# Turning 19 of 41 row tiles on VectorE instead of TensorE

## The chip, the core and the metric

The kernel runs on one core of a Trainium2 chip. TensorE (PE in the profile) multiplies matrices, VectorE (DVE), ScalarE (ACT) and GpSimd (POOL) work on tiles in SBUF, and transfers are issued from the queues of SP, ACT and POOL. The metric is the time of one execution on the device in microseconds (us), smaller being better.

## The reference

The input x has 2708 rows of 1024 numbers in fp32, and adj is a 2708 x 2708 matrix of zeros and ones in which a row has about four ones. What is computed:

```python
h = maximum(layernorm(x), 0)
q, k, v = h @ W_q.T + b_q, h @ W_k.T + b_k, h @ W_v.T + b_v
z = (q @ k.T) / sqrt(1024) * adj
z = where(z == 0, -10000, z)
out = x + relu(softmax(z, axis=1) @ v)
```

Only the scores at edges count, except in rows without edges, so the kernel does not form q @ k.T as a whole. It forms M = W_q.T W_k, multiplies the rows of h by M, takes for each row the dot products with the rows of h at its edges, sums those rows with the softmax weights into u, and multiplies u by W_v.

## The kernel before, in words

Rows are worked on in tiles of 128, 22 in all, the last with 20 rows. There are four stretches of work, which overlap on different engines.

*The weights.* W_q and W_k are loaded in eight tiles of 128 rows each. TensorE forms M by a scheme of Strassen's kind with seven products of half blocks (`term`, L460, line L463; banks `ps_x`, `ps_y`, `ps_z`), ScalarE evicts it (`evicted`, L476), VectorE adds parts to it (`joined`, L479) and forms differences of its blocks, called T, in `wlow` (`ts_of_m`, L425, L431). The host gives each weight row in an order that is not that of the columns: column c * 128 + p stands at place 8p + c. Block c of M's rows is therefore the columns c * 128 to c * 128 + 127, read with a step of eight elements (`a_tile`, L451), and evictions put M's columns back in order (`place`, `taken`, L467 to L474).

*The search.* Tiles of adj are loaded, VectorE looks for the ones with `max_index` (`found`, L376), lists them (`listed`, L389 to L395), counts them (`counts`, L645 to L653), and sorts the rows by their number of edges (`sort`, L666 to L673, ending with `pos_i`). POOL writes each row's list of edges to its sorted place in DRAM (`put`, L613) and the table is read back (`reload`, L625). This is done twice: for tiles 8 to 21, and then for tiles 0 to 7. Meanwhile h is normalised tile by tile and stored in `h_dram` (L270).

*Units.* A loop runs over 20 units, each a pair of row tiles: units 0 to 9 multiply rows of h by M and give q, units 10 to 19 multiply rows of u by W_v and give the output; one row tile, number 8, is left alone at the end. A unit is again seven products of half blocks (`multiply`, L982, line L948), and it needs its rows turned, with the columns in the partitions. For this TensorE multiplies 128 x 128 blocks with an identity (`half_turned`, L397, L402, bank `pt`), ScalarE copies them out (`held`, L682, L684), and VectorE and POOL form four sums and differences, s1 to s4 (`put`, L686, L688). `blocks` gives two steps, `upper` and `lower`, which are called in the unit before at given steps i of `after(i)` (L1172). The tiles of units 0 to 3 are those of h as they lie in SBUF (`kept`, `natural_rows`); units 4 to 9 gather their rows in sorted order from `h_dram` (`load_rows`, L1130, tiles `qr`); units 10 to 19 take u either from SBUF (`held`) or, when it was ready three units ahead or more, from `u_dram`, to which it was stored (`near`, L933). Ten tiles went through `u_dram`: 6, 5, 4, 3, 2, 0, 1, 20, 18 and 19.

*Attention.* For each sorted tile POOL gathers rows of h, one for each edge (L597), VectorE takes dot products with q (`scores`, L826), and sums the gathered rows with their weights into u (`sums`, L879), the first of them by ScalarE (`weights`, L871). It is a stream of steps (`attention`, L897) that is advanced between the steps of the units, by a fixed share for each step (`advance`). The order of the tiles is 6, 5, 4, 3, 2, 0, 1, 7, 13, 12, 11, 10, 14, 9, 15, 16, 20, 17, 18, 19, 8.

The order of VectorE's instructions is that of the program from beginning to end, and so is that of ScalarE's until unit 4 (`manual_schedule`, L413, L1164) and of POOL's in parts. An instruction that waits holds up all that follow on its engine. TensorE, SP and the rest are ordered by a planner when the kernel is built. The steps of the search stand in two tables, `steps_at` and `steps_ahead` (L735 to L740), with unit and step as keys. The kernel's helper `owe` (L278) adds rows into `hsum` on POOL at times when VectorE is not working on two operands.

After the last unit a flag tells whether any row had more edges than there is room for; only then does a slow general version of the whole follow, which does not run with this input.

## Time and profile before

| | |
|---|---|
| time, median of 3 runs | 647.9 us (647.47 to 648.41) |
| span of the profiled execution, first to last instruction | 641.9 us |
| time beyond the span (median less span) | 6.0 us |
| TensorE busy | 635.2 us, 1731 matmuls |
| VectorE busy | 521.9 us |
| POOL busy | 377.3 us |
| ScalarE busy | 279.6 us |
| moved by DMA | 189.02 MB, 294 GB/s in the mean |

The profiled execution's own time is not listed beside its span; the three timed runs stand within 0.15% of each other, and their median less the span is taken as what lies around it. In rows of groups the columns are line, engine, operation, output and inputs with shapes and count, then the busy time in us and the mean of one in ns, then the idle time before them and who ended it. In a timeline they are start, length, engine, line, operation, and in brackets the idle time before. In a table of stages they are the stage, its length, and the busy time of PE, PEld (TensorE's weight loads), DVE, ACT and POOL with the numbers of instructions, the granted clock of TensorE, the share of the DMA engines and GB/s. In rows of waits they are the total, how many times, and the longest.

### The profile page before, as it was taken

The page shows a single profiled execution, that of the slowest core. Times are in us where ns is not written, and L with a number is a line of the kernel's source. Part 1 is how long each engine was busy: PE and PEld are TensorE (multiplying, and loading weights), DVE is VectorE, ACT ScalarE, POOL GpSimd, SP SyncE. Part 2 cuts the span into 40 slices and gives each one's busy share as a digit, 9 for nine tenths or more (in the row PEclk, how much of TensorE's full clock was granted, in tenths as well). Part 3 has the DMA queues.
Part 4 walks back from the last instruction along what each step waited for, and adds up shares of the span by engine and source line. Part 5 has one row for each costly group of instructions (what it writes and reads, how often), then busy time and mean ns, then how long its engine had stood idle before and what let it go on. Part 6 is the DMA issues. An engine that isn't in the chain of part 4 may idle for free.

```text
span 641.9 us, 6381 instructions
## 1 busy us (share of the span) xinstructions
PE 635.2 (99%) x1731; PEld 326.2 (51%) x1731; DVE 521.9 (81%) x1014; ACT 279.6 (44%) x426; POOL 377.3 (59%) x400
## 2 busy tenths in 40 slices
PE   9999999999999999999999999999999999999996
PEld 5777766444544444444444454454454444444442
DVE  5999788997895755998888959997999989989121
ACT  3539974849775622423223132433342344333300
POOL 2649960875858457755735525665685856872431
PEclk9999999999999999999999999999999999999999
DMA  8999997598798969998977998988898989995542
GB/s 338 407 366 314 345 346 295 189 358 301 264 358 317 363 201 404 355 359 257 322 260 275 419 416 267 327 272 255 240 328 272 283 331 304 281 285 125 146 139 95
DMA packets 61986, 189.02 MB, mean 294 GB/s; under 512 B 10701, under 2 KB 11037, under 8 KB 61048
## 3 DMA queue, kind: packets, MB, share of 16 engines
q0 software_dynamic: 27888, 84.95, 41.6%
q1 hardware_dynamic: 29994, 89.36, 37.7%
q10 hardware_dynamic: 4062, 14.24, 5.9%
q8 instruction: 16, 0.26, 0.2%
q14 instruction: 26, 0.21, 0.1%
HBM read 159.81 MB, written 42.31 MB: 315 GB/s over the span
## 4 chain that ended last, share of the span: by engine, by line
PE 98%; DMA 1%; DVE 0%; POOL 0%; POOLq 0%; issue 0%
PE ps L948 45%; PE psy L948 32%; PE ps_y L463 6%; PE pt L402 6%; PE ps_x L463 4%; PE ps_z L463 4%; DMA wlow<-in_wq_dram 1%; PE ps_h L1153 0%; PE ps_v L581 0%; DVE y_alone L1297 0%; POOL out_dram L1281 0%; POOLq L1303 0%; PE ps_all L664 0%; PE ps_in L662 0%; PE ps_b L728 0%
## 5 line engine op out<-in xcount | busy, mean ns | idle before, releaser
L597 POOL DMA_INDIRECT g<-h_dram,tab x105 | 124.8, 1188 | 70.4 <-ACT u L871 19.1
L948 PE MATMUL ps<-M,a 128*128 128x512 f32 x320 | 144.0, 593 | 0.0
L948 PE MATMUL psy<-wlow,s 128*128 128x512 f32 x320 | 143.9, 592 | 0.0
L826 DVE SCALAR_TENSOR_TENSOR junk<-g,pq 128x1024 uint8<-128x1024 f32 x93 | 114.0, 1226 | 9.8 <-DMA g<-h_dram,tab 7.3
L879 DVE SCALAR_TENSOR_TENSOR u<-g,coef,u 128x1024 f32<-128x1024 f32 x79 | 101.4, 1283 | 5.6 <-ACT u L871 3.7
L948 PEld LDWEIGHTS ps<-M,a 128*128 128x128 f32 x320 | 59.3, 190 | 68.0 <-issue 67.4
L948 PEld LDWEIGHTS psy<-wlow,s 128*128 128x128 f32 x320 | 59.2, 190 | 66.8 <-issue 65.8
L376 DVE FIND_INDEX8 at<-ones,adj 128x8 uint32<-128x685 f32 (+1 forms) x88 | 74.5, 865 | 0.0
L948 PE MATMUL psy<-wlow,a 128*128 128x512 f32 x160 | 71.9, 592 | 0.0
L948 PE MATMUL ps<-M,s 128*128 128x512 f32 x160 | 71.9, 592 | 0.0
L948 PE MATMUL ps<-wlow,s 128*128 128x512 f32 x160 | 71.9, 592 | 0.0
L355 ACT ACTIVATE sized<-adj 128x2708 uint8<-128x2708 f32 (+1 forms) x22 | 54.3, 2468 | 7.7 <-DMA adj<-in_adj_dram 6.4
L285 POOL TENSOR_TENSOR hsum<-hsum,x 128x256 f32<-128x256 f32 (+1 forms) x56 | 38.6, 726 | 26.3 <-DVE wlow L431 22.3
L1047 POOL DMA_INDIRECT y<-in_x_dram,tab x19 | 33.5, 1763 | 30.8 <-ACT taken L1013 11.2
L948 PEld LDWEIGHTS psy<-wlow,a 128*128 128x128 f32 x160 | 30.4, 190 | 38.3 <-issue 37.8
L948 PEld LDWEIGHTS ps<-wlow,s 128*128 128x128 f32 x160 | 30.4, 190 | 38.3 <-issue 37.6
L948 PEld LDWEIGHTS ps<-M,s 128*128 128x128 f32 x160 | 30.3, 190 | 38.1 <-issue 37.4
L778 POOL DMA_INDIRECT out_dram<-y,tab x21 | 28.4, 1353 | 19.3 <-DMA y<-in_x_dram,tab 11.6
L684 ACT COPY a<-pt 128x512 f32<-128x512 f32 x60 | 33.4, 590 | 3.1 <-PE pt L402 3.1
L597 POOL DMA_INDIRECT M<-h_dram,tab x20 | 24.2, 1212 | 13.4 <-ACT u L871 4.7
L688 DVE TENSOR_TENSOR s<-a,pt 128x512 f32<-128x512 f32 x40 | 25.6, 681 | 7.8 <-ACT a L684 7.8
L871 ACT ACTIVATE u<-g,coef 128x1024 f32<-128x1024 f32 x16 | 18.4, 1149 | 27.1 <-DVE coef L870 26.3
(238 smaller groups left out, 847.9 us busy)
## 6 DMA issues: line engine op xcount, KB each, us to landing
adj<-in_adj_dram SPq DMA_DIRECT2D x21, 1354.0 KB, 12.0
x<-in_x_dram SPq DMA_DIRECT2D x21, 512.0 KB, 8.0
h_dram<-x ACTq DMA_DIRECT2D x21, 512.0 KB, 7.2
q_late<-q SPq DMA_DIRECT2D x12, 512.0 KB, 6.9
pq<-q_late SPq DMA_DIRECT2D x12, 512.0 KB, 4.8
u_dram<-u SPq DMA_DIRECT2D x10, 512.0 KB, 6.5
or<-u_dram SPq DMA_DIRECT2D x10, 512.0 KB, 8.2
g<-in_wv_dram SPq DMA_DIRECT2D x16, 256.0 KB, 8.3
```

The lines of the kernel that those rows point to most:

```text
L285: small.append(nc.gpsimd.tensor_add(hsum[:n, cols], hsum[:n, cols], xt[:n, cols]))
L355: nc.scalar.activation(sized[:n], a[:n, :, :PW], AF.Abs, accum_out=total[:n, t:t + 1])
L376: nc.vector.max_index(at[:n, k - first_k, g, :], ones[:n, 0:8], a[:n, g, :])
L402: nc.tensor.transpose(pt[:, c, :], xt[:, k * P:(k + 1) * P], ident)
L463: mm = nc.tensor.matmul(bank, a_tile(o + H * a[0], a[1], i), b(o), start=first and o == 0, stop=(o == H - 1), skip_group_check=True)
L597: return nc.gpsimd.indirect_dma_start(out=dst, out_offset=None, in_=src, in_offset=off, bounds_check=N - 1, oob_is_err=False)
L684: nc.scalar.copy(ops[name], bank)
L778: to = nc.gpsimd.indirect_dma_start(out=out, out_offset=bass.IndirectOffsetOnAxis(ap=ptab.bitcast(U32)[:n, t, SLOTS:SLOTS + 1], axis=0), i ...
L826: chained(lambda: nc.vector.scalar_tensor_tensor(junk, g_of[t][s], 1.0, tq[t], op0=ALU.mult, op1=ALU.mult, accum_out=zall[:, t, s:s + 1]))
L879: chained(lambda: nc.vector.scalar_tensor_tensor(u, g_of[t][s], coef[:, at[t][s]:at[t][s] + 1], u, op0=ALU.mult, op1=ALU.add))
L948: mm = nc.tensor.matmul(bank, a[:, c, :], b[:, c, :], start=False, stop=(c == 3), skip_group_check=True)
L1047: return nc.gpsimd.indirect_dma_start(out=y[:n], out_offset=None, in_=x, in_offset=off, compute_op=ALU.add)
```

## The change

Nineteen row tiles are no longer turned by TensorE. VectorE turns them in blocks of 32 x 32 with its own transpose (`faces`). Since such a block stays within 32 partitions, the rows come by four loads, one for each quarter of the partitions (`by_quarters`): quarter a gets columns 256a to 256a + 255 of all 128 rows, 32 rows side by side. The transpose reads every eighth column, so that partition p of block c holds column 8p + c. The weights are given plainly, and with the same step of eight as before their block c is now the columns 8p + c; M is evicted without being put in another order.

- Tiles 0 to 7 of h, in units 0 to 3, are loaded by quarters from `h_dram` (`quarter_rows`), not taken from SBUF. Both tiles of unit 0 are turned whole, ahead of part of `ts_of_m`; the others by halves.
- Tiles 6, 5, 4, 3, 2, 0, 1, 20, 18, 19 and 8 of u (`FACED`) are loaded by quarters from `u_dram`. Ten of them were stored and loaded before; tile 8 was not.
- The 12 tiles of units 4 to 9 come by gathers. ScalarE puts their columns in the order of the blocks (`combed`), and TensorE turns them as before. The other ten tiles of u are put in that order as they are summed (`combing`): u is written, and read back, at a step of 128 elements.
- s2 and s4 are formed by POOL for every pair with a tile that VectorE turned, in units 1 to 3 and in six of the later pairs; before, by POOL in units 1 and 2 alone. In unit 0 VectorE forms them, as before.
- `upper` and `lower` are called at other steps in units 0 to 2.
- `steps_at` is unchanged.

```diff
-P = 128
+P = 1024
+LANES = 128
+QUADS = 4
+FACED = (6, 5, 4, 3, 2, 0, 1, 20, 18, 19, 8)
+    def by_quarters(dst, rows):
+        faced.append(dst)
+        for a in range(QUADS):
+            cols = slice(a * D // QUADS, (a + 1) * D // QUADS)
+            nc.sync.dma_start(dst[a * QP:(a + 1) * QP, :].rearrange("r (g j) -> r g j", g=QUADS),
+                              rows[:, cols].rearrange("(g r) j -> r g j", r=QP))
+        return dst
+    def faces(dst, xt, lo, hi):
+        return nc.vector.transpose(dst.rearrange("p c (g r) -> p g c r", r=QP),
+                                   xt.rearrange("p (g r c) -> p g c r", g=QUADS, c=DC)[:, :, lo:hi])
+    def combed(xt, name):
+        c = row_tile(name)
+        nc.scalar.copy(c.rearrange("p (c q) -> p c q", c=DC), xt.rearrange("p (q c) -> p c q", c=DC))
+        return c
+    def combing(u, t):
+        return apart(u) if t in FACED else u.rearrange("p (c q) -> p q c", c=DC)
...
         def upper():
-            held("a11", half_turned(xa, 0))
-            held("a12", half_turned(xa, 1))
+            xa, xb = rows
+            if whole:
+                for xt, pair in ((xa, ("a11", "a12")), (xb, ("s3", "a22"))):
+                    wide = work.tile([P, D], FT, tag="q", name="turned", bufs=4).rearrange("p (c q) -> p c q", q=P)
+                    faces(wide, xt, 0, DC)
+                    ops[pair[0]], ops[pair[1]] = wide[:, :4], wide[:, 4:]
+                return
+            for s, name in enumerate(("a11", "a12")):
+                if is_faced(xa):
+                    faced_half(name, xa, s)
+                else:
+                    held(name, half_turned(xa, s))
...
-        ts_of_m(0, 0)
-        ts_of_m(1, 0, 1, 2, 3)
+        quarter_rows(0)
+        ts_of_m(0, 1)
         follow("i7.0-1")
+        ops_of[0] = blocks(rows_of.pop(0), whole=True)
+        ops_of[0][1]()
+        ts_of_m(2)
...
-ops_of[0][1]()
 ops_of[0][2]()
 banks_of = {0: banks_for(bp_sb)}
-    ts_of_m(0, 1, 3, 2)
+    ts_of_m(3)
...
             chained(lambda: nc.vector.scalar_tensor_tensor(
-                u, g_of[t][s], coef[:, at[t][s]:at[t][s] + 1], u, op0=ALU.mult, op1=ALU.add))
+                v, apart(g_of[t][s]), coef[:, at[t][s]:at[t][s] + 1], v, op0=ALU.mult, op1=ALU.add))
...
-                if i == (3 if n == 0 else 4 if turn else 0):
-                    ops_of[n + 1] = blocks(*rows_of[n + 1], nc.gpsimd if n + 1 < FIRST - 1 else None)
+                if i == {0: 3, 1: 3, 2: 2, FIRST - 1: 4}.get(n, 0):
+                    ops_of[n + 1] = blocks(rows_of[n + 1], nc.gpsimd if n + 1 < FIRST - 1 or any(
+                        is_faced(xt) for xt in rows_of[n + 1]) else None)
-                if i == (4 if n == 0 else 5 if turn else 2):
+                if i == {0: 4, 1: 4, 2: 3, FIRST - 1: 5}.get(n, 2):
                     ops_of[n + 1][2]()
...
+                if nxt[0] == "q" and n + 1 >= FIRST:
+                    if i == (3 if n + 1 == FIRST else 1):
+                        rows_of[n + 1][1] = combed(rows_of[n + 1][1], "cr")
+                    if n + 1 == FIRST and i == 2:
+                        rows_of[n + 1][0] = combed(rows_of[n + 1][0], "cr")
+                if i == 6 and n + 2 < len(units) and n + 2 > FIRST and units[n + 2][0] == "q":
+                    rows_of[n + 2][0] = combed(rows_of[n + 2][0], "cr")
```

176 lines of the change are left out of this document (91 added, 85 removed).

## The prediction

> **What bounds the kernel now.** I read the page's first parts for the bound, then the chain of waits in order of time, then each engine stage by stage for what comes just in time. Times are in us, from the start of the span.
>
> ```profile
> span 641.9 us, 6381 instructions
> PE 635.2 (99%) x1731; PEld 326.2 (51%) x1731; DVE 521.9 (81%) x1014; ACT 279.6 (44%) x426; POOL 377.3 (59%) x400
> ```
> ```profile
> 505.88 0.87 PE pt L402 x8
> ```
> ```profile
> 619.16 3.60 PE L948 MATMUL ps<-M,T_alone 128*128 128x512 f32 x8
> ```
>
> The first fence is the page, the second one row of the chain of waits, the third one of TensorE's timeline. TensorE is never without work, 99% of the span, and the turns of a row tile (pt, 8 of them, 0.87) lie in the chain. So an instruction taken from it is worth its full length, as long as everything else comes earlier by as much. The question is whether the others can. The runs had 647.47 to 648.41, median 647.9: 6.0 above the span. My sums are made on the span, and 6.0 is added.
>
> Two places have almost no slack. The first is the search for edges. Its table must be in DRAM before the rows of unit 4 can be gathered:
>
> ```profile
> 157.89 0.17 DVE L673 CAST pos_i<-deg 128x14 uint32<-128x14 f32 x1
> ...
> 192.70 1.07 POOL L599 DMA_INDIRECT qr<-h_dram,tab  x1 [2.38 <-DMA h_dram<-x]
> ```
> ```profile
> 200.43 1.05 PE L402 MATMUL pt<-ident,qr 128*128 128x128 f32 x8
> ...
> 205.63 1.88 PE L948 MATMUL ps<-M,a 128*128 128x512 f32 x4
> ```
> ```profile
> DMA to landing us min/median/max: 7.6/8.3/9.7
> ```
> ```profile
> 113.50:158.40 44.90, 44.90 (x126) 21.08 (x126) 40.36 (x110) 34.92 (x43) 34.34 (x59) 1.00 0.78 274
> 345.50:503.00 157.50, 157.50 (x446) 75.46 (x445) 140.83 (x213) 52.25 (x94) 93.27 (x71) 1.00 0.93 313
> ```
>
> The gather issued at 192.70 lands after 7.6 at the soonest, at 200.3, and TensorE turns its rows at 200.43: the slack is 0.1. Back from there it is one chain: table writes on POOL, the rows of the last tiles normalised and stored, all behind pos_i at 157.89. VectorE (third engine column of the stages) works 40.36 of 44.90 ahead of that, so pos_i comes when VectorE is through.
>
> The second place is the attention sums, 140.83 of 157.50 on VectorE. The last sum of tile 9 and of tile 8:
>
> ```profile
> 499.03 3.93 DVE L879 SCALAR_TENSOR_TENSOR u<-g,coef,u 128x1024 f32<-128x1024 f32 x3
> ...
> 590.13 1.28 DVE L879 SCALAR_TENSOR_TENSOR u<-g,coef,u 128x1024 f32<-128x1024 f32 x1
> ```
>
> Tile 9 is ready at 502.96 and turned at 505.88: slack 2.9. Tile 8 is ready at 591.4, its first block at 619.2.
>
> **The change, part by part.** *TensorE.* 19 tiles x 0.87 = 16.5 go: 8 in units 0 to 3, 7 (6.1) for the pairs of tiles 6,5 to 1,7, and 4 (20, 18, 19, 8; 3.5) at the end. If nothing waits: 631.4.
>
> *The price of a turn on VectorE.* No row shows one. It reads every eighth fp32 element, a stride of 32 bytes.
>
> ```profile
> L672 DVE TENSOR_REDUCE deg<-sort 128x14 f32<-128x252 f32 x1 | 0.6, 591 | 0.0
> L672 DVE TENSOR_REDUCE deg<-sort 128x8 f32<-128x144 f32 x1 | 0.4, 416 | 0.0
> L517 DVE TENSOR_SCALAR acc_b<-wlow,bq_sb 128x1024 f32<-128x1024 f32 x1 | 0.8, 753 | 0.0
> L688 DVE TENSOR_TENSOR s<-a,pt 128x512 f32<-128x512 f32 x40 | 25.6, 681 | 7.8 <-ACT a L684 7.8
> L431 DVE TENSOR_TENSOR wlow<-M,wlow 128x1024 f32<-128x1024 f32 x4 | 4.9, 1222 | 0.1
> ```
>
> L672 reads SBUF at strides of 56 and 32 bytes: (591 - 416) / (252 - 144) = 1.62 ns an element and 183 fixed, so a half tile of 512 takes 1.01 and a whole one 1.84. L517, one dense operand, is the cheap end: 0.75 a tile. I take L672, the row with the stride.
>
> *Search chain.* Unit 0 turns two whole tiles (3.7), units 1 and 2 four halves each (8.1): 11.8 ahead of pos_i. One L431 more comes ahead of the searches behind it (1.2). And VectorE waits, in order, for the first loads by quarters:
>
> ```profile
> 100.68 0.87 DVE L376 FIND_INDEX8 at<-ones,adj 128x8 uint32<-128x685 f32 x1
> ```
> ```profile
> 87.36 1.06 ACTq L270 DMA_DIRECT2D h_dram<-x  x2
> ```
> ```profile
> adj<-in_adj_dram SPq DMA_DIRECT2D x3, 1354.0 KB, 14.1
> h_dram<-x ACTq DMA_DIRECT2D x6, 512.0 KB, 3.6
> ```
> ```profile
> u_dram<-u SPq DMA_DIRECT2D x10, 512.0 KB, 6.5
> or<-u_dram SPq DMA_DIRECT2D x10, 512.0 KB, 8.2
> ```
>
> The stores of h end at 88.4 + 3.6 = 92.0. A load that takes 8.2 is there at 100.2, one that shares the queue with the adj loads (14.1) at 106.1; VectorE comes at 101.5. The wait is 0 to 4.6, and I take 2.5. Behind it on VectorE stand the searches, bp_sb and s1; behind the eight issues on SP the next adj loads, which VectorE does not need while it is itself late. Of the 4.5 idle before 158.4 I let 3.5 be used up. pos_i comes 2.5 + 11.8 + 1.2 - 3.5 = 12.0 later (2.2 with 0.75 a tile and no wait; 17.6 with the full wait and no idle used). Under this TensorE also loses its 7.0 of units 0 to 3: it gets to unit 4 early or on time, and waits.
>
> *Combing.* Rows from gathers are now first rearranged by ScalarE, 12 tiles. For unit 4 this stands in ScalarE's fixed order, so that behind the wait for the gather come the copies that free and fill the PSUM banks.
>
> ```profile
> 197.20 0.59 ACT L1026 COPY q<-ps 128x512 f32<-128x512 f32 x1 [2.85 <-PE ps L948]
> 197.68 1.11 ACT L713 COPY ps<-bp_sb 128x512 f32<-128x512 f32 x2
> 198.72 2.46 ACT L355 ACTIVATE sized<-adj 128x2708 uint8<-128x2708 f32 x1
> 201.09 0.19 ACT L355 ACTIVATION_READ_ACCUMULATOR sized<-adj 128x1 f32 x1
> 201.18 1.06 ACT L684 COPY a<-pt 128x512 f32<-128x512 f32 x2
> ```
> ```profile
> L871 ACT ACTIVATE u<-g,coef 128x1024 f32<-128x1024 f32 x16 | 18.4, 1149 | 27.1 <-DVE coef L870 26.3
> ```
>
> From the landing: comb 1.15, L1026 0.59, L713 1.11, comb 1.15, L355 2.65, first L684 0.53, together 7.2. Before it was 205.6 - 200.3 = 5.3. So unit 4 opens 12.0 + 1.9 = 13.9 late (4.1 to 19.5), and the attention stream with it: its own table is made from L688 of the same unit onward. The later combs are hidden by ScalarE's idle time (44% busy); without it each costs 1.15.
>
> *Attention stream.* From 345.5 to 503 VectorE gets 7 tiles x 2.02 = 14.1. The sums s2 and s4 of four pairs go to POOL: -8 x 0.69 = -5.5. But POOL's operations hold up VectorE's with two operands:
>
> ```profile
> 32.60 3.84 POOL L543 TENSOR_TENSOR wq<-wq,wlow 128x512 f32<-128x512 f32 x2 [3.45 <-DMA adj<-in_adj_dram]
> ```
> ```profile
> 33.02 5.83 DVE L519 SCALAR_TENSOR_TENSOR acc_b<-wk,bq_sb,acc_b 128x1024 f32<-128x1024 f32 x3
> ```
>
> Three operations of the kind that takes 1.28 alone (L879 above) took 5.83 beside two POOL operations: +1.0 for each, +8.0 for eight. POOL itself is 59% busy and hides the work; uncovered, each gather behind is 1.9 late (3.84 / 2). Of the waits in that stretch
>
> ```profile
> DVE junk L826 <- DMA g<-h_dram,tab: 7.3, 5, 2.1
> DVE s L688 <- ACT a L684: 3.4, 2, 2.2
> DVE u L1063 <- PE ps L948: 1.7, 1, 1.7
> ```
>
> a later VectorE meets none: -12.4. Net 4.2. The low end is 0 (an early VectorE still waits for its gathers). The sums of the ten tiles that TensorE still turns now read and write u at a stride of 512 bytes; I take 1.28 each, as now, and put the high end under the rivals.
>
> *Costed at nothing.* M is evicted straight, in as many instructions or fewer, in a stretch whose end TensorE sets. The weights' rows lie 32 KB apart instead of together, still 4 KB each: 0 to a few tenths at the start. The copies from PSUM that ScalarE no longer makes free an engine that is busy 44%. Loads by quarters have four issues and 1 KB runs; for tiles 6 to 1 and 20, 18, 19 they replace loads that are there (x10 above), well ahead of use.
>
> *Sum.* Tile 9 is ready 13.9 + 4.2 later, its slack of 2.9 is used, and the four last turns give 3.5 back: 13.9 + 4.2 - 2.9 - 3.5 = +11.7. The span is 653.6 and the time 659.6; I say 660. What is late next is the wait for u in the pair 14,9, while VectorE runs full.
>
> **The rivals.**
>
> *The turns hide, and it is faster.* With 0.75 a turn and no wait for the first loads unit 4 opens 4.1 late. The stream adds 0: 4.1 - 2.9 - 3.5 = -2.3, 645.6; if the sums too come in time, 4.1 - 9.6 = -5.5, 642.4. It decides in the search, ahead of pos_i: faster by over 0.2% needs delay and net stream work under 6.4 - 1.3 = 5.1 together. For it speak L517 and the 4.5 idle before 158.4; against it 40.36 of 44.90 and the slack of 0.1.
>
> *Strided sums.* At L672's rate a sum takes 1.84, not 1.28. Tiles 7, 13, 12, 11, 10, 14 and 9 have 2, 4, 4, 5, 5, 3 and 6 sums: 29 x 0.56 = 16.2 on a full engine. Then 659.6 + 16.2 = 675.8. The weight loads speak for it:
>
> ```profile
> L463 PEld LDWEIGHTS ps_y<-wlow 128*128 128x128 f32 x64 | 20.0, 313 | 7.4
> L948 PEld LDWEIGHTS ps<-M,a 128*128 128x128 f32 x320 | 59.3, 190 | 68.0 <-issue 67.4
> ```
>
> L463 takes its columns 32 bytes apart, L948 side by side: 313 against 190 ns. Against it: no row shows an operation with two operands at such a stride, and writes may not suffer. [...]
>
> *Tile 8 comes last.* It now goes through DRAM. VectorE ends it at 591.4 + 18.1 + some 5 (three more tiles turned) = 614.5; store 6.5, load 8.2, turn 1.84: 631.0. TensorE gets there at 619.2 + 15.2 - 2.6 = 631.8, just behind. With a load that takes 14.1 it waits 5.1 and the time is 664.7.
>
> **How the numbers follow.** About 0.2%, 1.3 us, is what a measurement of this kernel can tell from no change. Forecast (650 to 664) 0.43; tile 8 last 0.10; strided sums 0.25; faster 0.18; within 0.2% 0.04. So faster 0.18, same 0.04, slower 0.78. The range, 643 to 684, leaves out about 0.1 on each side; the forecast's own is 650 to 664.
>
> **What would show it.** Right: a gap on TensorE before its first turns of gathered rows, pos_i near 170, combs on ScalarE that wait for the gather, turns near 1.0 for 512, VectorE close to 100% from 350 to 500, TensorE waiting for u. Wrong: turns of 0.4, pos_i before 162, a chain that is still TensorE from end to end. L879 with a form at 1.8 would make it the second rival.

## The result, and the profile after

| kernel | median, us | lowest to highest | ratio to before, 95% interval |
|---|---|---|---|
| before | 648.15 | 647.47 to 649.79 | 1 |
| changed | 708.23 | 706.35 to 709.88 | 1.093 (1.0904 to 1.0956) |

The change is 9.3% slower, 60 us. The profiled execution of the changed kernel took 706.35 us with a span of 704.6, so 1.75 lies around the span and not 6.0: the profiled execution of before, with its span of 641.9, was some 4 us shorter than the timed ones.

The page after: its span, its busy times, and the granted clock in the 40 slices of the span:

```profile
span 704.6 us, 6216 instructions
PE 642.9 (91%) x1579; PEld 316.3 (45%) x1579; DVE 587.8 (83%) x1027; ACT 296.0 (42%) x408; POOL 417.9 (59%) x414
PEclk9999997999979999999999989999999899999999
```

The 152 blocks are gone from TensorE (1731 to 1579), and yet it is busy for longer: 642.9 after 635.2. Taken with the 16.5 us that were removed, the remaining work has become 24.2 slower. Idle it was for 641.9 - 635.2 = 6.7 and is now for 704.6 - 642.9 = 61.7. These two, 7.7 and 55.0, are the whole 62.7 by which the span grew. What TensorE waited for (us in total, times, longest):

```profile
PE ps L989 <- DVE s L470: 12.3, 3, 5.3
PE ps L989 <- DVE a L454: 9.7, 1, 9.7
PE psy L989 <- ACT taken L1054: 7.8, 6, 3.3
PE psy L989 <- DMA wlow<-tv_dram: 4.7, 1, 4.7
PE pt L406 <- DVE u L920: 4.7, 2, 4.4
...
PE pt L406 <- ACT cr L752: 3.7, 3, 2.3
```

TensorE's waits of this kind add up to 56.0 us. VectorE itself ended 36.2 of them, copies of ScalarE 13.9. How the lateness grew, read from the timelines of both kernels at the same places:

| place | before | after | later by |
|---|---|---|---|
| pos_i of tiles 8 to 21 | 157.89 | 173.12 | 15.2 |
| gather of unit 4's rows issued | 192.70 | 212.25 | 19.6 |
| first turn of unit 4 | 200.43 | 223.07 | 22.6 |
| first turn of unit 9 | 319.20 | 346.94 | 27.7 |
| first turn of the pair 13,12 | 449.84 | 485.52 | 35.7 |
| first turn of the pair 15,16 | 527.20 | 588.44 | 61.2 |
| end of the span | 641.9 | 704.6 | 62.7 |

So three stretches matter most: units 0 to 3 (22.6), the gathered rows (5.1), and the units of u, above all between the pairs 13,12 and 15,16 (25.5). TensorE's gaps in the first stretch, from its timeline (start, length, what, and in brackets the idle time before and who ended it):

```profile
108.47 5.37 PE L989 MATMUL ps<-M,turned 128*128 128x512 f32 x8 [3.92 <-DVE turned L454]
119.13 5.60 PE L989 MATMUL ps<-wlow,s 128*128 128x512 f32 x8 [5.30 <-DVE s L470]
...
162.28 0.27 PE L726 MATMUL ps_in<-sort,before 128*128 128x252 bf16 x1 [3.21 <-DVE sort L714]
...
199.87 6.19 PE L989 MATMUL ps<-M,a 128*128 128x512 f32 x8 [9.74 <-DVE a L454]
...
223.07 1.04 PE L406 MATMUL pt<-ident,cr 128*128 128x128 f32 x8
```

The gaps are 3.9, 5.3, 3.2 and 9.7, and each of the three long ones is followed by a block that takes 5.4 to 6.2 in place of 3.60. At unit 4 itself (the last row) TensorE does not wait at all. The costliest rows of VectorE and ScalarE that are new or have changed, from the groups:

```profile
L920 DVE SCALAR_TENSOR_TENSOR u<-g,coef,u 128x1024 f32<-128x1024 f32 x79 | 128.4, 1625 | 9.1 <-ACT u L911 7.2
L911 ACT ACTIVATE u<-g,coef 128x1024 f32<-128x1024 f32 x16 | 25.0, 1560 | 33.0 <-DVE coef L910 27.6 <-DVE m L909 5.2
L752 ACT COPY cr<-qr 128x1024 f32<-128x1024 f32 x12 | 24.8, 2067 | 27.6 <-DMA qr<-h_dram,tab 27.6
L920 DVE SCALAR_TENSOR_TENSOR u<-M,coef,u 128x1024 f32<-128x1024 f32 x13 | 21.0, 1614 | 2.4 <-ACT u L911 2.1
L454 DVE STREAM_TRANSPOSE a<-or 128x512 f32<-128x512 f32 x16 | 17.0, 1088 | 0.0
L454 DVE STREAM_TRANSPOSE turned<-hq 128x1024 f32<-128x1024 f32 x2 | 4.0, 2016 | 6.2 <-DMA hq<-h_dram 6.2
```

The means of L920 and L911 mix two kinds: sums of tiles in FACED take 1.28, those of the other ten tiles some 2.02, as this row of VectorE's timeline shows (six in a row, 12.13):

```profile
545.27 12.13 DVE L920 SCALAR_TENSOR_TENSOR u<-g,coef,u 128x1024 f32<-128x1024 f32 x6
```

### The profile page after: what moved, and what is told of

Read it like the earlier page. It is cut to its first block, busy times and chain, and to the rows that moved or that the text cites. A ratio compares the mean times of both kernels' runs of the same rounds, so it can differ in the third digit from the quotient of the medians.

```text
span 704.6 us, 6216 instructions
## 1 busy us (share of the span) xinstructions
PE 642.9 (91%) x1579; PEld 316.3 (45%) x1579; DVE 587.8 (83%) x1027; ACT 296.0 (42%) x408; POOL 417.9 (59%) x414
## 4 chain that ended last, share of the span: by engine, by line
DVE 36%; PE 22%; issue 16%; DMA 13%; ACT 5%; POOL 5%; SPq 1%; ACTq 0%; another core or an unknown queue 0%; POOLq 0%; DVEq 0%
DVE u L920 11%; DVE junk L858 8%; PE ps L989 7%; PE psy L989 5%; DVE at L380 4%; PE ps_x L540 4%; DMA adj<-in_adj_dram 3%; DMA g<-h_dram,tab 3%; DMA qr<-h_dram,tab 3%; DVE s L470 3%; DVE a L454 2%; PE ps_y L540 2%; PE ps_z L540 2%; POOL g L662 2%; DMA tv_dram<-g 2%
## 5 line engine op out<-in xcount | busy, mean ns | idle before, releaser
L662 POOL DMA_INDIRECT g<-h_dram,tab x105 | 136.1, 1296 | 72.6 <-ACT u L911 29.6
L989 PE MATMUL ps<-M,a 128*128 128x512 f32 x304 | 141.5, 609 | 9.7 <-DVE a L454 9.7
L920 DVE SCALAR_TENSOR_TENSOR u<-g,coef,u 128x1024 f32<-128x1024 f32 x79 | 128.4, 1625 | 9.1 <-ACT u L911 7.2
L858 DVE SCALAR_TENSOR_TENSOR junk<-g,pq 128x1024 uint8<-128x1024 f32 x93 | 116.7, 1255 | 4.0 <-DMA pq<-q_dram,tab 1.4
L989 PE MATMUL ps<-wlow,s 128*128 128x512 f32 x160 | 77.5, 630 | 12.3 <-DVE s L470 12.3
L1088 POOL DMA_INDIRECT y<-in_x_dram,tab x19 | 35.3, 1856 | 20.8 <-ACT y L1105 9.9
L911 ACT ACTIVATE u<-g,coef 128x1024 f32<-128x1024 f32 x16 | 25.0, 1560 | 33.0 <-DVE coef L910 27.6
L752 ACT COPY cr<-qr 128x1024 f32<-128x1024 f32 x12 | 24.8, 2067 | 27.6 <-DMA qr<-h_dram,tab 27.6
L662 POOL DMA_INDIRECT M<-h_dram,tab x20 | 26.1, 1306 | 13.7 <-ACT u L911 5.6
L746 ACT COPY ps<-bp_sb 128x512 f32<-128x512 f32 x42 | 24.6, 595 | 16.2 <-DVE bp_sb L652 7.9
```

The lines of the kernel that those rows point to most:

```text
L662: return nc.gpsimd.indirect_dma_start(out=dst, out_offset=None, in_=src, in_offset=off, bounds_check=N - 1, oob_is_err=False)
L752: nc.scalar.copy(c.rearrange("p (c q) -> p c q", c=DC), xt.rearrange("p (q c) -> p c q", c=DC))
L858: chained(lambda: nc.vector.scalar_tensor_tensor(junk, g_of[t][s], 1.0, tq[t], op0=ALU.mult, op1=ALU.mult, accum_out=zall[:, t, s:s + 1]))
L911: nc.scalar.activation(combing(u, t), apart(g_of[t][0]), AF.Copy, scale=coef[:, at[t][0]:at[t][0] + 1])
L920: chained(lambda: nc.vector.scalar_tensor_tensor(v, apart(g_of[t][s]), coef[:, at[t][s]:at[t][s] + 1], v, op0=ALU.mult, op1=ALU.add))
L989: mm = nc.tensor.matmul(bank, a[:, c, :], b[:, c, :], start=False, stop=(c == 3), skip_group_check=True)
```

## The experiments

All times are medians, and the ratio is to the kernel before on the same chip. What a part is worth is taken from the ratios, times 648.15, unless the text says that it goes by medians.

| run | what | us | ratio, 95% interval |
|---|---|---|---|
| e1_sums | changed, sums plain | 679.99 | 1.0464 (1.0442 to 1.0487) |
| e2_rows | changed, gathered rows not rearranged | 704.61 | 1.0845 (1.0821 to 1.0870) |
| e3_first | changed, units 0 to 3 turned by TensorE | 690.29 | 1.0622 (1.0583 to 1.0660) |
| e4_layout | plain weights alone | 649.82 | 1.0003 (0.9986 to 1.0020) |
| e5_u_faces | plain weights, 11 tiles of u turned by VectorE | 657.17 | 1.0129 (1.0101 to 1.0156) |
| e6_queue | changed, loads of h on ScalarE's queue | 722.51 | 1.1125 (1.1096 to 1.1153) |
| e7_order | changed, sums of unit 0 ahead of the search | 709.51 | 1.0938 (1.0914 to 1.0961) |
| e8_last_faces | plain weights, tiles 20, 18, 19 | 650.50 | 1.0028 (1.0008 to 1.0047) |
| e9_loads | plain weights and unused loads of h | 652.98 | 1.0063 (1.0041 to 1.0084) |
| e10_turns | plain weights and unused turns | 654.61 | 1.0087 (1.0061 to 1.0113) |
| e11_fewer | e5 without tiles 4 and 3 | 654.27 | 1.0096 (1.0067 to 1.0125) |
| e12_late | plain weights, tiles 18, 19, 8, turned late in order | 647.21 | 0.9983 (0.9973 to 0.9994) |
| e13_ahead | changed, turns of unit 3 ahead of the search | 707.46 | 1.0914 (1.0861 to 1.0967) |
| e14_vector | e5, s2 and s4 by VectorE | 654.60 | 1.0095 (1.0066 to 1.0123) |
| e15_prices | e4 and 21 single operations | 672.8, once | |
| e16_full | e12 and tile 20 | 655.76 | 1.0103 (1.0080 to 1.0127) |

### The parts taken back one at a time

Sums plain (`apart` leaves the order as it is). TensorE turns a tile by every eighth column, unless its columns were rearranged (`in_blocks`):

```diff
 def combing(u, t):
-    return apart(u) if t in FACED else u.rearrange("p (c q) -> p q c", c=DC)
+    return apart(u)
...
 def half_turned(xt, s):
...
-            nc.tensor.transpose(pt[:, c, :], xt[:, k * P:(k + 1) * P], ident)
+            block = xt[:, k * P:(k + 1) * P] if any(xt is y for y in in_blocks) else \
+                xt.rearrange("p (q c) -> p q c", c=DC)[:, :, k]
+            nc.tensor.transpose(pt[:, c, :], block, ident)
```

> The changed kernel, but u is summed plainly for all tiles (no step of 128 elements), and TensorE reads the ten tiles that it still turns by every eighth column. Theory A (the sums at a step of 512 bytes cost the most behind unit 12): every sum takes 1.28 again, VectorE loses 31 us of busy time, and most of the lateness that grew from 36 to 61 us between the pairs 13,12 and 15,16 goes: 708 becomes 676 to 690. Rival B (VectorE is full there by the turns and by POOL's s2 and s4, the sums only share the blame): no more than 10 us come back, 698 or more. If TensorE's turns suffer from the step of 32 bytes, up to 10 us are lost again and the rows of the turns show it.

It fell from 1.093 to 1.0464, by 4.7% or 30 us, inside Theory A's range. VectorE's rows of the sums in this run:

```profile
L923 DVE SCALAR_TENSOR_TENSOR u<-g,coef,u 128x1024 f32<-128x1024 f32 x79 | 106.2, 1344 | 8.9 <-ACT u L914 7.0
L923 DVE SCALAR_TENSOR_TENSOR u<-M,coef,u 128x1024 f32<-128x1024 f32 x13 | 16.7, 1283 | 1.5 <-ACT u L914 1.2
```

They take 122.9 where the changed kernel takes 149.4: 26.5 less VectorE, and about as much less time. In the changed kernel VectorE is busy 182.74 of the 190 us from 400 to 590, and TensorE, which was busy all the time before, 166.72:

```profile
400.00:590.00 190.00, 166.72 (x404) 74.78 (x403) 182.74 (x245) 60.95 (x96) 122.69 (x79) 0.93 0.83 256
```

The traced execution of this run is the slowest of its five (688.91); even there the pair 15,16 is 42.6 late and not 61.2.

Rows of units 4 to 9 straight from the gathers, turned by TensorE as above:

```diff
-                if nxt[0] == "q" and n + 1 >= FIRST:
-                    if i == (3 if n + 1 == FIRST else 1):
-                        rows_of[n + 1][1] = combed(rows_of[n + 1][1], "cr")
...
-                    rows_of[n + 2][0] = combed(rows_of[n + 2][0], "cr")
```

> The changed kernel without the rearranging of the gathered rows by ScalarE: TensorE turns the 12 tiles of units 4 to 9 by every eighth column. Theory A (lateness before unit 4 comes from units 0 to 3, the combs add only what the lateness grows from unit 4 to unit 9, 22.6 to 27.7): about 5 us come back, 700 to 706. Rival C (the chain gather, comb, turn is what opens unit 4 late, as the prediction had it): unit 4 opens 2 or more earlier and with it all behind, the gain is 2 to 4 at unit 4 and up to 12 x 2.07 = 25 in all.

1.0845, so 0.85% or 5.5 us come back (3.6 by the medians), on either side of the 5.1 in the table of lateness: Theory A. The much larger gain of Rival C is not there.

Units 0 to 3 from the rows in SBUF, as before the change:

```diff
-        quarter_rows(0)
         ts_of_m(0, 1)
         follow("i7.0-1")
-        ops_of[0] = blocks(rows_of.pop(0), whole=True)
-        ops_of[0][1]()
...
-                    quarter_rows(n + 2)
+                    natural_rows(n + 2)
```

> The changed kernel, but units 0 to 3 take the rows of h from SBUF again and TensorE turns them (every eighth column); no loads of h by quarters. Theory A (the gaps of 3.9, 5.3, 3.2 and 9.7 us in units 0 to 3 and the slower first blocks behind them make unit 4 22.6 late, and all of it is carried to the end): 708 becomes 682 to 689. Rival D (VectorE is the bound from 345 to 600 in any case and takes most of the gain back): 695 to 706.

1.0622: 3.1% or 20 us (17.9 by the medians). 690.29 lies between the two ranges, 1.3 above Theory A's and 4.7 below Rival D's: most of what units 0 to 3 lose, 22.6 by the table, is carried to the end.

All three, and nothing turned by VectorE:

```diff
-FACED = (6, 5, 4, 3, 2, 0, 1, 20, 18, 19, 8)
+FACED = ()
...
-                faces(uT, single["rows"], 0, DC)
+                for s in range(2):
+                    nc.scalar.copy(uT[:, 4 * s:4 * s + 4], half_turned(single["rows"], s))
```

> No tile is turned by VectorE, no row is rearranged, no sum is written apart: what is left of the change is the plain order of the weights, and TensorE turns all 41 tiles by every eighth column. Theory A (the three causes above are all there is): 646 to 652, like the kernel before. Rival E (the plain weights or the step of 32 bytes under TensorE's turns cost by themselves): 653 or more, and the rows of the weights' loads or of the turns are longer than before.

649.82, ratio 1.0003: the plain weights cost nothing that the interval of 0.2% to either side can show. TensorE's weight loads when it turns columns 32 bytes apart (first row, this run) and columns side by side (second row, the kernel before), and those of `term`, which read at a step of 32 bytes in both kernels (last row, this run):

```profile
L410 PEld LDWEIGHTS pt<-ident,qr 128*128 128x128 f32 x96 | 12.4, 191 | 7.2 <-issue 7.2
L402 PEld LDWEIGHTS pt<-ident,qr 128*128 128x128 f32 x96 | 11.1, 141 | 5.9 <-issue 5.9
L540 PEld LDWEIGHTS ps_y<-wlow 128*128 128x128 f32 x64 | 20.1, 313 | 7.4
```

With the step these loads take 191 and not 141. They run beside the matmuls, and a turn of eight blocks takes TensorE hardly longer, 1.04 to 1.06 and not 1.04. What makes the loads of `term` 313 stays open. Neither the rearranging by ScalarE nor the sums at a step were needed for TensorE's sake.

### The turns of u

What was left of the change beside those three parts, by itself (the diff is from e4):

```diff
-FACED = ()
+FACED = (6, 5, 4, 3, 2, 0, 1, 20, 18, 19, 8)
...
-                for s in range(2):
-                    nc.scalar.copy(uT[:, 4 * s:4 * s + 4], half_turned(single["rows"], s))
+                faces(uT, single["rows"], 0, DC)
```

> Only the eleven tiles of u in FACED are turned by VectorE, with their loads by quarters and POOL's s2 and s4; units 0 to 3 are turned by TensorE from SBUF, nothing is rearranged, every sum is plain. The three parts taken back one at a time gave 28.2, 3.6 and 17.9 of the 58.4 us between the changed kernel and the plain layout; 8.7 are left. Theory A (the parts add up, and the faces of u themselves are a loss: the wait of 4.7 for a table load of W_v behind the quarter loads, the slower clock behind it, POOL beside VectorE): 655 to 662. Rival F (with VectorE free of the other parts, these turns hide and TensorE is 11 x 0.87 = 9.6 shorter): 640 to 646.

1.0129, a loss of 1.3% or 8 us though TensorE has 9.6 less to do. With e1, e2 and e3 (30, 5.5 and 20 us) the parts make 64 us, against 60 for the whole: they add up to within the intervals of four measurements. The largest gap of this run, and the DMA traffic ahead of it in the run with the turns of u and in e4 (a stage, its length, busy times and numbers, granted clock, DMA share, GB/s), in this order:

```profile
392.57 6.39 PE L982 MATMUL psy<-wlow,s 128*128 128x512 f32 x8 [5.05 <-DMA wlow<-tv_dram]
```
```profile
360.00:370.00 10.00, 10.00 (x25) 4.42 (x24) 9.79 (x9) 0.00 (x0) 8.19 (x6) 1.00 1.04 328
```
```profile
360.00:370.00 10.00, 10.00 (x25) 4.50 (x24) 9.86 (x12) 1.18 (x2) 7.26 (x6) 1.00 1.03 423
```

Both have the DMA engines full, but with quarter loads among the transfers they move 328 GB/s and not 423. Behind them a table of W_v comes late: 5.05 of waiting, and a block of 6.39 in place of 3.60. To see whether the quarter loads of tiles 4 and 3 make it late, e11 leaves them out (the diff is from e5):

```diff
-FACED = (6, 5, 4, 3, 2, 0, 1, 20, 18, 19, 8)
+FACED = (6, 5, 2, 0, 1, 20, 18, 19, 8)
```

> Turns of u alone, as in the run that gave 657.2, without tiles 4 and 3: these are loaded plainly and turned by TensorE. Their eight quarter loads were issued between the loads of W_v, for the last of which TensorE waited 5.1 and then ran 2.8 slower. Theory L (the 1 KB runs of these loads make the loads of W_v late): wait and slow blocks go, 1.7 of turns come back, 649 to 652. Rival (the wait comes from the late store of q ahead of them in SP's queue, or from elsewhere): 656 to 660.

The wait for W_v is gone from its trace, and the stage from 360 to 370 moves 421 GB/s again, as Theory L says; but the time is 1.0096, 2 us less and not 5 to 8, outside both ranges, and the intervals of e5 and e11 overlap. Nor is Theory L shown, since its rival, the store of q ahead in SP's queue, stands in the traces too. SP's timeline in e5, and then in e11:

```profile
370.26 0.34 SPq L1056 DMA_DIRECT2D q_late<-q  x1
370.69 0.93 SPq L1287 DMA_DIRECT2D M<-in_wv_dram  x2
```
```profile
357.79 3.77 SPq L1287 DMA_DIRECT2D M<-in_wv_dram  x2
369.37 0.33 SPq L1056 DMA_DIRECT2D q_late<-q  x1
```

In e5 two loads of W_v stand behind the store of q, for which SP's queue waited 12.3 us until VectorE had formed q; in e11 they stand ahead of it and are issued 10 to 13 us earlier. In the changed kernel they stand behind it as well (394.14, a wait for q of 12.2). So two things differ between the runs, the runs of 1 KB and this order, and the two rates above are of different traffic. That the turns of tiles 4 and 3 bring the wait is shown: the traces of all nine kernels that have them wait 3.9 to 5.1 for this table, and no other does. By which way, and what it is worth, is not.

s2 and s4 back on VectorE (the diff is from e5):

```diff
-                    ops_of[n + 1] = blocks(rows_of[n + 1], nc.gpsimd if n + 1 < FIRST - 1 or any(
-                        is_faced(xt) for xt in rows_of[n + 1]) else None)
+                    ops_of[n + 1] = blocks(rows_of[n + 1], nc.gpsimd if n + 1 < FIRST - 1 else None)
```

> Turns of u alone (657.2), with s2 and s4 of the later pairs formed by VectorE, not by POOL. The prediction put each operation of POOL at 1.0 lost on VectorE beside it and each of VectorE's own at 0.69. If that is right, VectorE's busy time falls by some 12 x 0.3 = 4 us and the time with it, 653 to 656. If POOL's operations mostly fall beside work that they do not hold up: 657 to 662.

654.60 is in the first range, though again the intervals overlap, so the gain itself is not shown; VectorE is busy 543.0 and not 546.1. How POOL holds up an operation shows in the changed kernel's timelines: two that take 1.22 and 1.28 alone, and POOL's beside them.

```profile
415.23 2.29 DVE L858 SCALAR_TENSOR_TENSOR junk<-M,pq 128x1024 uint8<-128x1024 f32 x1
417.45 2.27 DVE L920 SCALAR_TENSOR_TENSOR u<-g,coef,u 128x1024 f32<-128x1024 f32 x1
```
```profile
414.74 1.70 POOL L470 TENSOR_TENSOR s<-s,a 128x512 f32<-128x512 f32 x1 [0.57 <-DVE s L470]
416.52 2.12 POOL L470 TENSOR_TENSOR s<-a,s 128x512 f32<-128x512 f32 x1
```

### Units 0 to 3: loads, work or order

Loads of h by quarters from ScalarE's queue:

```diff
-    def by_quarters(dst, rows):
+    def by_quarters(dst, rows, queue=nc.sync):
...
-            rows_of[n].append(by_quarters(xt, h_dram[t * P:(t + 1) * P, :]))
+            rows_of[n].append(by_quarters(xt, h_dram[t * P:(t + 1) * P, :], nc.scalar))
```

> The changed kernel, with the loads of h by quarters issued from ScalarE's queue, not from SP's, so that the loads of adj do not stand behind them. Theory G (adj late by the queue: VectorE's 4.4 idle at 188 and part of the 9.7 gap of TensorE ahead of unit 3 come from it): VectorE's waits for adj fall from 12.6 to below 8, 700 to 705. Rival (the loads are late by the DMA engines or their buffers, not by the queue): 706 to 710.

1.1125, 12.6 us slower than the change, outside both ranges. Its waits show why it tells nothing on the question: ScalarE itself now stood idle at these loads (two waits of 13.0 and 12.7), and VectorE's waits for adj rose from 12.6 to 17.3. Theory G is neither shown nor refuted by it.

In unit 0, s1 to s4 ahead of the searches:

```diff
         ops_of[0][1]()
-        ts_of_m(2)
...
-                follow("f7.2-3")
...
     ops_of[0][2]()
     banks_of = {0: banks_for(bp_sb)}
-    ts_of_m(3)
+    ts_of_m(2, 3)
+    follow("f7.2-3")
```

> The changed kernel, but in unit 0 VectorE forms s1 to s4 ahead of the differences of M and of the two searches that stood before them. The gap of 5.3 at 119 us and the 2.0 of slower blocks behind it go. Theory H (VectorE's amount of work up to the turns of unit 3 sets when unit 4 opens): the gap moves to a later turn, 705 to 709. Rival I (the order alone makes that part of the delay): 699 to 703.

709.51, the change's time: Theory H. The gap of 5.3 at 119 is gone, and one of 6.1 stands at 137, where the next unit's turned tile is awaited.

In unit 2, the turns of unit 3's tiles at steps 0 and 1, not 2 and 3:

```diff
-                if i == {0: 3, 1: 3, 2: 2, FIRST - 1: 4}.get(n, 0):
+                if i == {0: 3, 1: 3, 2: 0, FIRST - 1: 4}.get(n, 0):
...
-                if i == {0: 4, 1: 4, 2: 3, FIRST - 1: 5}.get(n, 2):
+                if i == {0: 4, 1: 4, 2: 1, FIRST - 1: 5}.get(n, 2):
```

> The changed kernel, but in unit 2 VectorE turns the tiles of unit 3 at steps 0 and 1, ahead of the searches of steps 1 to 3, not at steps 2 and 3. TensorE waited 9.7 for these tiles at 190 us and ran 2.6 slower behind it. Theory M (what units 0 to 3 lost beyond the loads, 3.9, and VectorE's extra work, 5.4, comes from turned tiles that stand in VectorE's order behind searches which wait for adj): most of that gap goes, 696 to 702. Rival H (VectorE's amount of work alone sets it, as in unit 0, where the order did nothing): the gap comes back at the next unit, 705 to 709.

707.46, ratio 1.0914: no difference from the change, so Rival H. TensorE's timeline, where the changed kernel had its gap of 9.74:

```profile
195.34 3.67 PE L989 MATMUL ps<-M,a 128*128 128x512 f32 x8 [3.10 <-DVE a L454]
...
207.56 5.29 PE L989 MATMUL psy<-wlow,a 128*128 128x512 f32 x8 [4.76 <-DVE q L1070]
```

The turned tile is there earlier, and TensorE waits two blocks later for the next thing in VectorE's order. Twice, then, the order was changed and the time was not.

The loads alone, into tiles that nobody reads, beside the plain layout (the diff is from e4):

```diff
+        quarter_rows(0)
         ts_of_m(0, 1)
...
     natural_rows(1)
+    quarter_rows(1)
...
                     natural_rows(n + 2)
+                    quarter_rows(n + 2)
```

> The plain layout with all turns on TensorE (649.8), and beside it the 32 loads of h by quarters at their places in the first stage, into tiles that nobody reads. It prices the loads alone: SP's queue, the adj loads behind them and the DMA engines. Theory J (VectorE's work, not the loads, opens unit 4 late): 649 to 653. Rival K (the adj loads stand behind the loads of h and VectorE waits for them): 654 to 660.

1.0063, 0.6% or 3.9 us over e4: the upper end of Theory J's range. 2.9 of it is one slower block behind a gap of 3.5. VectorE's waits for adj rose from 17.3 in e4 to 20.0.

The turns alone, of tiles that are there anyway, beside the plain layout (from e4):

```diff
+        for k in range(2):
...
+            faces(wide, acc_b, 0, DC)
...
+                if n < 3 and i in ((3, 4), (3, 4), (2, 3))[n]:
...
+                    for s in range(2):
+                        faces(spare[:, 4 * s:4 * s + 4], bp_sb, 4 * s, 4 * s + 4)
```

> The plain layout with all turns on TensorE (649.8), and beside it the 2 whole and 12 half transposes of the first stage at their places in VectorE's order, of tiles that are there anyway, with results that nobody reads: 4.0 + 13.0 = 17.0 us more on VectorE, 12.7 of them ahead of pos_i, and no new wait. Theory H (little slack ahead of pos_i, VectorE's amount of work sets the opening of unit 4): 9 to 13 us later, 659 to 663. Rival (VectorE's idle time takes them in): 650 to 654.

1.0087, 0.84% or 5.4 us over e4, between the two ranges. pos_i came at 165.70, against 158.43 in e4: of the 12.7 ahead of it 5.4 fell into idle time. So neither the loads nor the work explains 20 us alone. In the change both come together, with a wait that the work alone does not have: VectorE stands idle until the first quarter loads have landed. That what it then has left to do no longer finds the idle time that hid 5.4 here is the likely reading, which no run tests by itself. VectorE's and POOL's timelines of the changed kernel, and one row of POOL's before:

```profile
106.32 2.01 DVE L454 STREAM_TRANSPOSE turned<-hq 128x1024 f32<-128x1024 f32 x1 [5.88 <-DMA hq<-h_dram]
...
173.12 0.17 DVE L737 CAST pos_i<-deg 128x14 uint32<-128x14 f32 x1
...
188.58 0.09 DVE L380 MATCH_VALUE_LOAD at<-ones,adj 128x8 f32 x1 [4.37 <-DMA adj<-in_adj_dram]
...
198.62 3.08 DVE L454 STREAM_TRANSPOSE a<-hq 128x512 f32<-128x512 f32 x3
...
204.66 0.68 DVE L1070 TENSOR_TENSOR q<-psy,p 128x512 f32<-128x512 f32 x1
```
```profile
206.57 5.53 POOL L289 TENSOR_TENSOR hsum<-hsum,x 128x256 f32<-128x256 f32 x8
212.25 1.07 POOL L664 DMA_INDIRECT qr<-h_dram,tab  x1 [0.15 <-issue]
```
```profile
184.80 5.52 POOL L285 TENSOR_TENSOR hsum<-hsum,x 128x256 f32<-128x256 f32 x8 [0.62 <-DVE q L1029]
```

These are the chain: 5.9 waited at 100, the turns, pos_i 15.2 late, 4.4 waited for adj, the four turns of unit 3, the addition of unit 2's q at 204.66, and only behind that the additions on POOL that `owe(8)` makes wait for it, and behind them the gather. Before (last row), these additions ended at 190.32, and the gather at 192.70 waited another 2.38 for the stores of h; now it follows them at once, 19.6 later. In the two orders that were tried the time did not change, so as far as they go it is the sum of VectorE's work and waits that counts. How the 20 us divide among wait, work and slower blocks is not settled, since they do not add when taken alone.

### The price of an operand at a step

```diff
+    added(gc, ga, gb)
+    added(by128(gc), apart(ga), by128(gb))
+    added(by128(gc), apart(ga), apart(gb))
+    added(apart(gc), apart(ga), by128(gb))
+    added(apart(gc), by128(ga), by128(gb))
+    added(by8(gc), ga.rearrange("p (c q) -> p c q", c=DC), by8(gb))
...
+    nc.vector.transpose(gc, ga)
```

> The plain layout with 16 operations of VectorE and 5 of ScalarE added behind the last unit, on three tiles in SBUF, each with another step of its operands; results that nobody reads. It prices the operations, its time is of no interest. A sum of 1024 with nothing apart takes 1.28, in the form of the change (read and written at 512 bytes) 2.0. Theory N: the step costs by the side on which it stands, and a sum that only writes apart, or only reads apart, shows which. If reading suffers: 1.9 for the one that reads apart and 1.3 for the one that writes apart; if writing suffers, the other way; if each costs its own part, both are between. ScalarE's copy: 2.07 in the form of the change, 1.15 dense. Transposes: 2.02 with the step of 32 bytes; if it is the step that costs, a dense one of 1024 takes 1.1 to 1.3.

From VectorE's timeline of this run: a sum with nothing apart; four at 512 bytes (output and one input, output alone, one input alone, both inputs), and the last of these four by itself; one at 32 bytes; a scaling of one input, dense and then with the output at 512 (with the input at 512 it took 1.25, at 32 bytes 1.08); then a turn of 1024 with the change's step and one without. Each form ran once.

```profile
633.81 1.27 DVE L1301 SCALAR_TENSOR_TENSOR g<-g,msq,g 128x1024 f32<-128x1024 f32 x1
...
635.12 8.56 DVE L1301 SCALAR_TENSOR_TENSOR g<-g,msq,g 128x1024 f32<-128x1024 f32 x4
...
641.23 2.45 DVE L1301 SCALAR_TENSOR_TENSOR g<-g,msq,g 128x1024 f32<-128x1024 f32 x1
...
644.07 2.18 DVE L1301 SCALAR_TENSOR_TENSOR g<-g,msq,g 128x1024 f32<-128x1024 f32 x1
...
651.34 0.69 DVE L1311 TENSOR_SCALAR g<-g 128x1024 f32<-128x1024 f32 x1
652.07 1.26 DVE L1312 TENSOR_SCALAR g<-g 128x1024 f32<-128x1024 f32 x1
...
656.87 2.01 DVE L454 STREAM_TRANSPOSE g<-g 128x1024 f32<-128x1024 f32 x1
658.91 1.25 DVE L1317 STREAM_TRANSPOSE g<-g 128x1024 f32<-128x1024 f32 x1
```

The first three of the four take 2.00 each: one operand apart costs as much as output and input together, whether it is read or written. With both inputs apart it is 2.45. At 32 bytes a sum takes 2.18, a tenth more than at 512. That is none of the three answers that the expectation offered. ScalarE's copy took 1.04 dense, and 1.91 to 2.02 in the four other forms. A turn takes 1.25 without the step: 0.76 of its 2.01 is the step.

### Where a turn is free

Tiles 20, 18 and 19 alone, with the steps of the change (the diff is from e4):

```diff
-FACED = ()
+FACED = (20, 18, 19)
```

> Only tiles 20, 18 and 19 are turned by VectorE, at the end, where it is busy 22 of 60 us; everything else is turned by TensorE, nothing is rearranged, every sum is plain. If turns are free where VectorE has time: 3 x 0.87 = 2.6 less than the plain layout, 646.5 to 648 against 649.8. If the loads by quarters or the sums on POOL come late there: 649 or more.

1.0028 (against 1.0003 for e4): no gain. TensorE waits 2.24 for a bank and the block behind takes 5.40: in VectorE's order the turns of the next unit stood ahead of the addition that empties a bank of the present one. With 18, 19 and 8 alone, s2 and s4 by VectorE as in e14, and the turns behind that addition (the diff is from e4):

```diff
-FACED = ()
+FACED = (18, 19, 8)
...
-                if i == {0: 3, FIRST - 1: 4}.get(n, 0):
...
+                if i == {0: 3, FIRST - 1: 4, len(units) - 2: 4}.get(n, 0):
...
-                if i == {0: 4, FIRST - 1: 5}.get(n, 2):
+                if i == {0: 4, FIRST - 1: 5, len(units) - 2: 5}.get(n, 2):
...
-            if nxt is None and i == 5:
+            if nxt is None and i == 4:
                 uT = work.tile([P, D], FT, tag="hT", name="T_alone", bufs=2)
```

> Only tiles 18, 19 and 8 are turned by VectorE, behind the last sums: those of 18 and 19 stand in VectorE's order behind the addition that frees the bank of the unit before, not ahead of it, tile 8 a step earlier than in the change; s2 and s4 are VectorE's. Everything else as in the plain layout (649.8). If turns are free where VectorE is idle and nothing that TensorE waits for stands behind them: 3 x 0.87 = 2.6 less, 646.5 to 648. If the sums of 18 and 19 come late behind their turns: 649 to 652.

0.9983 (0.9973 to 0.9994): faster than both kernels, by less than the 0.2% that the prediction called measurable, though the interval leaves out 1. It is the best that came of the change. Against e4 (0.9986 to 1.0020) the intervals overlap, and since e12 differs from e8 in three things (tile 8 for 20, who forms s2 and s4, the order), no run tells which of them helped. Tile 20 as well, at the same steps one unit earlier, where VectorE is still summing:

```diff
-FACED = (18, 19, 8)
+FACED = (20, 18, 19, 8)
...
-                if i == {0: 3, FIRST - 1: 4, len(units) - 2: 4}.get(n, 0):
+                if i == {0: 3, FIRST - 1: 4, len(units) - 2: 4, len(units) - 3: 4}.get(n, 0):
...
-                if i == {0: 4, FIRST - 1: 5, len(units) - 2: 5}.get(n, 2):
+                if i == {0: 4, FIRST - 1: 5, len(units) - 2: 5, len(units) - 3: 5}.get(n, 2):
```

> As the run with tiles 18, 19 and 8 that gave 647.2, and tile 20 as well, whose turn falls where VectorE is still full of sums (56.7 of 60 us before). If a turn is free only where VectorE has idle time, TensorE's 0.9 are more than lost again: 648 to 651. If not: 646.3.

1.0103, worse than e12 by 1.2%, and by more than was expected. One row of TensorE's timeline has it: VectorE's turn comes late, and the clock goes down: the run's page has it at 0.7 in the slice from 573 to 589, and at 0.8 or more in all others.

```profile
579.88 6.41 PE L982 MATMUL ps<-M,a 128*128 128x512 f32 x8 [5.14 <-DVE a L454]
```

## Why the prediction was wrong

*What bounds the kernel: right; what an instruction taken from TensorE is worth: not shown.* The 152 blocks went. In e12, where little else was in their way, TensorE's busy time is 2.3 below e4's, for three turns of 2.6; that the time falls as much is not shown, since e12 is 1.3 us below e4 by the ratios, with overlapping intervals.

*The price of a turn: nearly right.* 1.01 and 1.84 from L672; 1.09 and 2.02 measured.

*The wait for the first loads: mis-sized.* 2.5 was taken, with 4.6 as the bound; it was 5.9. The landing behind the bound, 106.1, was right to 0.2, though by another way: the eight quarter loads alone occupied SP's queue for 11.4 from 94.3. VectorE came earlier than assumed, at 100.4 and not 101.5.

*pos_i 12.0 late, unit 4 13.9 late: right in mechanism, too small.* pos_i came 15.2 later, inside the range given, unit 4 22.6, outside it (4.1 to 19.5). The step that failed is "Back from there it is one chain: table writes on POOL, the rows of the last tiles normalised and stored, all behind pos_i": the gather also stood behind `owe(8)`, which waits for an addition of VectorE that comes after unit 3's turns. Before, that way to the gather had 2.4 to spare; now it came last. So the four turns of unit 3 (4.2), and a wait of 4.4 for adj, loads that VectorE "does not need while it is itself late" (before, the longest such wait was 2.6), belonged to the chain.

*"It gets to unit 4 early or on time, and waits": wrong.* TensorE lost its time in units 0 to 3, 22 us in four gaps, three of them before tiles that now came late from VectorE, one before its sort. At unit 4 it did not wait.

*The combs: mis-sized and not hidden.* 2.07 where 1.15 was taken from a dense L871, and "the later combs are hidden by ScalarE's idle time" failed: undoing all twelve gave 5.5 us (3.6 by the medians). ScalarE is idle, but it waits for the gather, and TensorE for ScalarE.

*The attention stream, net 4.2: this is where the prediction broke.* The step is "I take 1.28 each, as now". A sum at a step took 2.02, and undoing that alone gave 30 us, half of the loss. It was the second rival, held at 0.25. That rival's price of 16.2 was too small too. In the trace 37 sums are at a step and not 29, since tiles 15, 16 and 17 have another eight, and each takes 0.73 more and not 0.56, 27 in all (VectorE's 26.5 less in e1); and TensorE's gaps brought the slower clock with them (0.93 granted from 400 to 590, where it was 1.00 before). Its evidence, 313 against 190, compares loads of two kinds; loads of one kind, those of the turns, show the step too (191 against 141, e4), but TensorE's weight loads do not price a sum. What it said against itself, that no row shows two operands at a step and that writes may not suffer, was the question that decided; e15 answers it.

*POOL holds VectorE up by 1.0 each: right*, by the rows above (2.29 for 1.22, 2.27 for 1.28); e14's 2 us are within the intervals. *-12.4 for waits that go: right.* Of the three kinds 0.9 is left on VectorE between 381 and 565.

*Quarter loads of u at nothing: wrong.* With those of tiles 4 and 3 a table of W_v came 4.7 late, and without them it did not (e11); whether their four issues in SP's queue or their runs of 1 KB did it is open, and so is what the time lost by it.

*-3.5 at the end: not there.* From the pair 15,16 to the end the lateness grew by 1.5; of the four turns nothing came back, as gaps of 0.7, 2.2 and 0.8 on TensorE took as much.

*Tile 8 last: did not happen*; no wait for its tile shows.

*Not in the prediction at all:* the clock. To 55.0 us more idle time TensorE's slower work adds 24.2, of which 18.6 stand, block by block against 3.60 (1.04 for turns), behind nine of its gaps.

The range reached to 684 since each rival was priced with all other terms at their middle; here the high ends came together, since all of them are late work of the one engine that was full.

## What to carry to other kernels

Work that moves from a full engine to a less full one must be priced with all that it needs there: here the turn itself was the small part, and the layout that it asked of other operations (sums and copies at a step) cost half the loss. Before any change of layout, price one operation of each kind with one operand at the new step; on VectorE and ScalarE one such operand made fp32 work of 1024 elements 0.4 to 1.0 us longer here, and TensorE's weight loads 50 ns, which its matmuls hid (a turn of eight blocks took 1.04 to 1.06 after 1.04). In one run alone (e12) did turns on VectorE lose no time: VectorE was idle there, and they stood in program order behind what frees TensorE's banks. One tile more, where VectorE was still summing (e16), cost 1.2%.

## What the runs showed of the hardware

*The clock after a gap.* Granted clock in stages of the changed kernel around the gap of 9.74 (a stage, its length, busy times, then the clock third from the end):

```profile
199.80:202.00 2.20, 2.13 (x3) 1.13 (x4) 2.20 (x3) 2.17 (x3) 0.00 (x0) 0.50 1.02 395
...
204.00:206.00 2.00, 2.00 (x5) 0.82 (x4) 2.00 (x5) 0.11 (x2) 1.92 (x2) 0.76 1.03 415
206.00:208.00 2.00, 2.00 (x6) 0.85 (x5) 2.00 (x7) 0.57 (x1) 2.00 (x4) 1.00 0.91 371
```

The granted clock is 0.50 from 199.80 to 204, 0.76 from there to 206 and 1.00 behind it: half clock for some 5 us behind this gap, and then full. Over the changed kernel and all the runs but the one of single prices, of 68 gaps of 0.6 to 1.87 us none was followed by slower blocks, behind 27 of 54 between 1.88 and 3.3 they came, and behind 46 of 47 longer ones; the loss was 1.3 to 1.8 us behind the former and 1.4 to 3.0 behind the latter, and a gap of 9.88 cost no more (2.95, e2) than one of 5.56 (2.98, e1). If the clock is the half behind every such gap, slow times are twice the loss, an estimate: 3.5 to 5.8 us in the changed kernel. What decides between the gaps of 1.88 to 3.3 no run shows. With nine slow stretches the changed kernel lost 18.6 of 704.6 us.

*One operand at a step of 32 or 512 bytes* made fp32 work of 1024 elements longer in e15, read or written: a sum on VectorE 2.00 to 2.2 against 1.27, a scaling 1.08 to 1.26 against 0.69, a copy on ScalarE 1.9 to 2.0 against 1.04. Output and one input together cost a sum no more than one of them, both inputs did (2.45, at 512 bytes).

*Weight loads of columns 32 bytes apart*, in TensorE's turns, took 191 ns against 141 side by side (e4 and before), and the turns themselves hardly longer (1.04 to 1.06 against 1.04).
